# Reordering the prologue of a two-layer attention kernel: transposes of z one tile ahead, x requested one tile sooner

## The chip, the cores and the metric

The kernel runs on one core of one Trainium2 chip. The metric is the device time of the whole program in microseconds (us), the median of several runs. All arithmetic is in 32-bit floats. The engines have short names in the profile: PE is TensorE (matmuls and transposes; PEld its weight loads), DVE is VectorE, ACT is ScalarE, POOL is GpSimd, SP is SyncE, whose queue issues most of the DMAs. Each engine works through its own instructions in the order in which the program gives them, and waits where one of them needs the result of another engine or a buffer that is still in use.

## The reference

`x` is 128 x 256 x 256 (rows s, positions i, channels), `z` is 256 x 256 x 128. Two layers follow each other; cut to what matters here:

```python
# layer 0: x = x + attention0(group_norm(x), z)
m_norm = layer_norm(m)                       # m = group_norm(x)
z_norm = layer_norm(z, eps=1e-5)             # over the 128 channels of z
q, k, v = m_norm @ Wq.T, m_norm @ Wk.T, m_norm @ Wv.T      # 8 heads of 32
b = (z_norm @ Wb.T).transpose(0, 3, 1, 2)[:, None]          # a bias for each head, i, j
scores = einsum('bsihc,bsjhc->bshij', q, k) * scale + b
p = softmax(scores)
# ... times v, gate, output matrix
# layer 1: x = x + attention1(group_norm(x)), banded, 4 heads of 64
```

`_gn` needs mean and variance of x over all rows and positions for each of 32 groups of channels, so all of x has to be read before layer 0 can start on its first row. The bias `b` is the same for all 128 rows s, so it is made once.

## The kernel before: the prologue

Before the main loop of layer 0 there is a prologue. It reads z in 16 tiles (`zjobs`, 2 MB each) and x in 8 blocks (4 MB each, `nga` is 8). For each tile of z: VectorE takes the variance of each row (`z_front`) and GpSimd turns it into 1/std by a power of -0.5; TensorE transposes the tile, ScalarE copies the transposed parts out of PSUM, and TensorE multiplies them with the weights of the bias (`z_back`, `z_project`). The mean need not be subtracted: the weights are centred instead. When two tiles (64 columns) are through, the result is transposed back into `ps_k`, VectorE multiplies it with 1/std, and ScalarE takes the exponential (`z_exp`), because the main loop multiplies by exp(b). For each block of x VectorE sums moments (`x_block`). Comments marked `#:` are added here.

```python
    def z_load(b, i0, parts=1):
        zt = pz.tile([P, IB, CZ], F32, name="zt", tag="zt", bufs=3)   #: three buffers
        ...
            nc.sync.dma_start(zt[:, part]..., z_rows[...])
        return zt

    def z_front(b, i0, zt):
        nonlocal zrs
        st = pz.tile([P, IB, 3], F32, name="zst", tag="zst", bufs=2)
        for i in range(0, IB, 2):                       #: 16 instructions
            if i % (IB // 4) == 0 and i:
                mark(i // (IB // 4))                    #: other work between the quarters, see plan
            nc.vector.bn_stats(...)
        at = i0 % IS
        if at == 0:
            zrs = pz.tile([P, IS], F32, name="zrs", tag="zrs", bufs=3)
        rs = zrs[:, at : at + IB]
        nc.vector.tensor_scalar(rs, st[:, :, 2], 1.0 / CZ, 1e-5, ALU.mult, ALU.add)
        nc.gpsimd.tensor_tensor(rs, rs, mhalf[:, :IB], ALU.pow)
        return zt, zrs

    def z_back(b, i0, zt, rs):
        nonlocal turned
        at = i0 % IS
        for j in range(at // 16, (at + IB) // 16):      #: two halves of a tile
            zTs = []
            for g in range(4):
                ps_t = pps.tile([P, 512], F32, name="ps_t", tag="zT", bufs=3)
                ...
                for a in range(4):
                    nc.tensor.transpose(ps_t[:, a * P : (a + 1) * P], zt[:, i + a, :], ident)
                zT = pz.tile([P, 512], F32, name="zT", tag="zT", bufs=10)
                nc.scalar.copy(zT, ps_t)
                zTs.append(zT)
            z_project()                                 #: of the half before
            turned = (b, i0 - at, rs, j, zTs)

    def z_project():
        ...
        for g in range(4):
            nc.tensor.matmul(ps_b[...], wbz[:, j]..., zTs[g], start=(j == 0), stop=(j == 3))
        if j == 1:
            z_exp()
        if j < 3:
            return
        bT = pz.tile([P, 512], F32, name="bT", tag="bT", bufs=2)
        nc.scalar.copy(bT, ps_b)
        ps_k = pps.tile([P, 4, 4, 4, H], F32, name="ps_k", tag="keys", bufs=1)
        for a in range(4):
            nc.tensor.transpose(ps_k[:, a]..., bT[:, a * P : (a + 1) * P], ident)
        bt = pz.tile([P, IS, H], F32, name="bt", tag="bt", bufs=2)
        for j in range(4):
            nc.vector.tensor_tensor(bt[...], ps_k[...], bcast(rs...), ALU.mult)
        weighed.append((b, i0, bt))

    def x_block(j):
        xa = px.tile([P, GA * NB, C], F32, name="xa", tag="xa", bufs=2)   #: two buffers
        nc.sync.dma_start(xa, x[j * GA : (j + 1) * GA]...)
        for g in range(0, G, 2):                        #: 16 instructions
            nc.vector.bn_stats(st0[:, j, g : g + 2, :]..., group_pairs(xa, g))
```

The work between the quarters of `z_front`: during tiles 1 and 6 it is steps of preparing the weights. After the last block of x (`ended`, tile 8) it is the plan below; a key gives how many tiles after that one, and after which quarter. `begin` and the two `next(steps)` make the moments of x (`gps` and `gps2` are small matmuls that average over the partitions, `rs_l` the root that GpSimd takes), `take`, `norm` and `weigh` start on the first rows of layer 0.

```python
    plan = {
        (0, 4): begin, (1, 1): lambda: next(steps), (1, 3): lambda: next(steps), (1, 4): take, (2, 3): norm,
        (3, 4): weigh,
        (5, 3): lambda: now.send(nc.scalar),            #: 1/std of the first rows to DRAM
        (6, 4): lambda: now.turn([mm("ps_x") for _ in range(KC)]),
        (7, 2): lambda: now.fetch(nc.scalar),           #: and back, on all partitions
        (7, 4): lambda: now.normal(),                   #: xnT, on GpSimd
    }
```

```python
    behind, nx, n = None, 0, 0
    prepare = weights()
    with tc.manual_schedule():                          #: each engine keeps the order of the program
        zts = [z_load(*zjobs[0], 2)]
        load(8)                                         #: small loads of weights, ScalarE's queue
        zts.append(z_load(*zjobs[1]))
        for n, job in enumerate(zjobs):
            front = z_front(*job, zts.pop(0) if zts else z_load(*job))
            if n == 0:
                next(prepare)
                next(prepare)
            else:
                load(4)
                if n == 1:
                    next(prepare)
            if behind is not None:
                z_back(*behind)                         #: of the tile before
            behind = (*job, *front)
            if nx < n and nx < nga:
                x_block(nx)
                nx += 1
                if nx == nga:
                    ended = n
            mark(4)
        assert not plan
        z_back(*behind)
        z_project()
        z_exp()
        now.project("qT", 0)                            #: then the main loop begins
        now.project("kT", 0)
        ...
```

Of the kernel before, what the change touches and what calls it, by code (L numbers as in the profile page):

```python
# [9 lines left out]
F32 = mybir.dt.float32  # L10
# [6 lines left out]
P = 128  # L17
# [4 lines left out]
def bcast(ap, axis, n):  # L22

    ap = ap.unsqueeze(axis)
    shape = list(ap.shape)
    shape[axis] = n
    return ap.broadcast_to(shape)
# [746 lines left out]
def fast_kernel(  # L774
# [28 lines left out]
    H = wbT.shape[1]  # L803
# [24 lines left out]
    queued = []  # L828

    def load(n):  # L830
        for _ in range(min(n, len(queued))):
            nc.scalar.dma_start(*queued.pop(0))
# [98 lines left out]
    for a in range(KC):  # L931
        for h in range(H1):
            n = P // H1
# [5 lines left out]
    for h in range(H1):  # L939
        n = P // H1  # L940
# [22 lines left out]
    def group_pairs(src, g):  # L963

        return src[:, :, g * GE : (g + 2) * GE].rearrange("p n (h e) -> p n e h", h=2)
# [30 lines left out]
    pps = tc.alloc_tile_pool(name="pre_ps", bufs=2, space=PSUM)  # L996

    def mm(name):
        return ps_mm.tile([P, 512], F32, name=name, tag="mm")
# [73 lines left out]
    nga = S // GA  # L1073
# [7 lines left out]
    zjobs = [(b, i) for b in range(NB) for i in range(0, I, IB)]  # L1081
# [3 lines left out]
    def z_load(b, i0, parts=1):  # L1085

        zt = pz.tile([P, IB, CZ], F32, name="zt", tag="zt", bufs=3)
        for u in range(parts):
            part = slice(u * IB // parts, (u + 1) * IB // parts)
            nc.sync.dma_start(  # L1090
                zt[:, part].rearrange("p (u b) c -> p u (b c)", b=NB),
                z_rows[b, :, (i0 + part.start) // NB : (i0 + part.stop) // NB, :],
            )
        return zt

    def z_front(b, i0, zt):
        nonlocal zrs

        st = pz.tile([P, IB, 3], F32, name="zst", tag="zst", bufs=2)
        for i in range(0, IB, 2):  # L1100
            if i % (IB // 4) == 0 and i:
                mark(i // (IB // 4))
            nc.vector.bn_stats(
                st[:, i : i + 2, :].rearrange("p i f -> p (i f)"),
                zt[:, i : i + 2, :].rearrange("p i c -> p c i"),
# [4 lines that stand above are left out]
        rs = zrs[:, at : at + IB]  # L1110
        nc.vector.tensor_scalar(rs, st[:, :, 2], 1.0 / CZ, 1e-5, ALU.mult, ALU.add)
        nc.gpsimd.tensor_tensor(rs, rs, mhalf[:, :IB], ALU.pow)
        return zt, zrs

    def z_back(b, i0, zt, rs):

        nonlocal turned
        at = i0 % IS
        for j in range(at // 16, (at + IB) // 16):
# [3 lines that stand above are left out]
                i = (4 * j + g) * 4 - at  # L1123
# [3 lines that stand above are left out]
                nc.scalar.copy(zT, ps_t)  # L1127
                zTs.append(zT)
            z_project()
            turned = (b, i0 - at, rs, j, zTs)  # L1130

    def z_project():
        nonlocal turned, ps_b
        if turned is None:
            return
        (b, i0, rs, j, zTs), turned = turned, None
        if j == 0:
            ps_b = pps.tile([P, 512], F32, name="ps_b", tag="bias", bufs=1)
        for g in range(4):
            nc.tensor.matmul(  # L1140
                ps_b[32 * g : 32 * (g + 1), :], wbz[:, j].rearrange("p a h -> p (a h)"), zTs[g],
                start=(j == 0), stop=(j == 3),
            )
        if j == 1:
            z_exp()
        if j < 3:
            return
        bT = pz.tile([P, 512], F32, name="bT", tag="bT", bufs=2)
        nc.scalar.copy(bT, ps_b)
        ps_k = pps.tile([P, 4, 4, 4, H], F32, name="ps_k", tag="keys", bufs=1)  # L1150
        for a in range(4):
            nc.tensor.transpose(
                ps_k[:, a].rearrange("p g j h -> p (g j h)"), bT[:, a * P : (a + 1) * P], ident
            )
        bt = pz.tile([P, IS, H], F32, name="bt", tag="bt", bufs=2)
        for j in range(4):
            q = slice(j * 16, (j + 1) * 16)
            nc.vector.tensor_tensor(
                bt[:, q, :].rearrange("p (g a) h -> p g a h", g=4), ps_k[:, :, :, j, :].rearrange("p a g h -> p g a h"),
                bcast(rs[:, q].rearrange("p (g a) -> p g a", g=4), 3, H), ALU.mult,  # L1160
            )
        weighed.append((b, i0, bt))

    def z_exp():

        while weighed:
            b, i0, bt = weighed.pop()
            for h in range(H):
                nc.scalar.activation(
                    eb[:, h, :, b * P + i0 // NB : b * P + (i0 + IS) // NB],  # L1170
                    bt[:, :, h].rearrange("p (u b) -> p b u", b=NB), AF.Exp, bias=bz_r[:, h : h + 1],
                )

    def x_block(j):
        xa = px.tile([P, GA * NB, C], F32, name="xa", tag="xa", bufs=2)
        nc.sync.dma_start(xa, x[j * GA : (j + 1) * GA].rearrange("s i c -> (s i) c").rearrange("(p n) c -> p n c", p=P))
        for g in range(0, G, 2):
            nc.vector.bn_stats(st0[:, j, g : g + 2, :].rearrange("p g f -> p (g f)"), group_pairs(xa, g))

# [273 lines left out]
    def pair(p):  # L1453
        return Pair(p) if p < NP else Nobody()

    turned, weighed = None, []
    zrs = ps_b = la = lb = ps_s = ps_o = M0 = R0 = None
    now = nxt = nn = None

# [22 lines left out]
    def weigh():  # L1482
# [6 lines left out]
# [3 lines that stand above are left out]
        (5, 3): lambda: now.send(nc.scalar),  # L1492
        (6, 4): lambda: now.turn([mm("ps_x") for _ in range(KC)]),
        (7, 2): lambda: now.fetch(nc.scalar),
        (7, 4): lambda: now.normal(),
    }
    ended = None

    def mark(quarter):
        if n == 1 and quarter < 4 or n == 6:  # L1500
            next(prepare, None)
        if ended is not None:
            plan.pop((n - ended, quarter), nothing)()


    behind, nx, n = None, 0, 0
    prepare = weights()
    with tc.manual_schedule():
        zts = [z_load(*zjobs[0], 2)]
        load(8)  # L1510
        zts.append(z_load(*zjobs[1]))
        for n, job in enumerate(zjobs):
            front = z_front(*job, zts.pop(0) if zts else z_load(*job))
            if n == 0:
                next(prepare)
                next(prepare)
            else:
                load(4)
                if n == 1:
                    next(prepare)  # L1520
            if behind is not None:
                z_back(*behind)
            behind = (*job, *front)
            if nx < n and nx < nga:
                x_block(nx)
                nx += 1
                if nx == nga:
                    ended = n
            mark(4)
        assert not plan  # L1530
        z_back(*behind)
        z_project()
        z_exp()
        now.project("qT", 0)
        now.project("kT", 0)
        for f in ("centre", "scale"):
            getattr(nxt, f)()
        for r in range(2):
            nxt.moments(r)
# [111 lines left out]
    with tc.tile_pool(name="l1", bufs=2) as sb, tc.tile_pool(  # L1651
        name="l1s", bufs=4
    ) as sm, tc.tile_pool(name="ps1_mm", bufs=2, space=PSUM) as ps_mm, tc.tile_pool(
        name="ps1_s", bufs=1, space=PSUM
# [236 lines left out]
@with_exitstack  # L1891
def mixer_kernel(ctx, tc, *args):

    nc = tc.nc
    keep = ctx.enter_context(tc.tile_pool(name="verdict", bufs=1))
    verdict = keep.tile([1, 1], mybir.dt.int32, name="verdict")
    fast_kernel(tc, *args, verdict)
    again = nc.values_load(verdict[0:1, 0:1], min_val=0, max_val=1)
    with tc.If(again > 0):
        general_kernel(tc, *args)  # L1900
# [53 lines left out]
```

## Time and profile before

| | |
|---|---|
| time, median of 3 runs | 3370.63 us (3367.43 to 3371.21) |
| profiled span | 3366.7 us, granted TensorE clock 0.983 |
| TensorE busy | 3221.6 us, 96% |
| VectorE busy | 2024.1 us, 60% |
| ScalarE busy | 1463.3 us, 43% |
| GpSimd busy | 1975.2 us, 59% |
| last block of x done | 161.1 us after the start |
| first scores of the main loop | 239.8 us after the start |

A line of the timeline reads: start and length in us, engine, source line, operation, tile written and tile read, shapes, the number of instructions merged, and in brackets how long the engine had been idle before it and what ended that. `SPq` is the queue of the SP engine: its lines are DMA requests, and their length is the time of asking, not of the transfer. In the view by windows, each engine has its busy time and, in brackets, its number of instructions; behind them are the granted clock, the busy share of the DMA engines and the rate.

### The profile page before, as it was taken

How to read it: one execution, taken by the hardware profiler on the slowest of the kernel's cores; microseconds unless marked ns; L12 is line 12 of the kernel's file. 1: busy time of each engine (PE TensorE's matmuls, PEld its weight loads, DVE VectorE, ACT ScalarE, POOL GpSimd, SP SyncE). 2: the span in 40 equal slices, each digit the busy share in tenths (PEclk: the TensorE clock that was granted, in tenths of full speed). 3: DMA queues.
4: the chain of work that ended last, by engine and by line, in shares of the span. 5: the costliest groups of instructions: out<-in, count | busy, mean ns of one | idle time of the engine just before them, and what ended most of it. 6: DMA issues, size and time to landing. Idle time of an engine off the chain costs nothing. (4 is left out here: it accounts for less than half of the span.)

```text
span 3366.7 us, 81193 instructions
## 1 busy us (share of the span) xinstructions
PE 3221.6 (96%) x35158; PEld 2032.1 (60%) x35158; DVE 2024.1 (60%) x3218; ACT 1463.3 (43%) x2121; POOL 1975.2 (59%) x1377
## 2 busy tenths in 40 slices
PE   5389999999999999999999998899999999999998
PEld 3245555555555555555555554567767777677676
DVE  7966666666666666666666666366544444443456
ACT  2264444444444444444444443344444444444443
POOL 2378787777777787887777874333333333333332
PEclk8699999999999999999999999999999999999999
DMA  9951212221222222122212221211211211212111
GB/s 351 367 136 43 72 49 73 74 73 48 73 74 60 55 71 68 48 73 74 74 49 73 74 63 45 68 58 53 64 53 52 65 53 55 62 52 62 56 57 53
DMA packets 198831, 262.91 MB, mean 78 GB/s; under 512 B 46304, under 2 KB 147552, under 8 KB 197312
## 3 DMA queue, kind: packets, MB, share of 16 engines
q1 hardware_dynamic: 193392, 254.72, 24.8%
q8 instruction: 279, 4.57, 0.7%
q10 hardware_dynamic: 5072, 2.90, 0.3%
q14 instruction: 88, 0.72, 0.1%
HBM read 188.82 MB, written 68.75 MB: 77 GB/s over the span
## 5 line engine op out<-in xcount | busy, mean ns | idle before, releaser
L1344 POOL TENSOR_TENSOR eboth<-e 128x512 f32<-128x512 f32 x512 | 640.4, 1272 | 389.4 <-DVE e L1339 389.4
L1339 DVE TENSOR_TENSOR e<-ps_sc,eb 128x1024 f32<-128x1024 f32 x512 | 603.0, 1219 | 316.4 <-ACT ps_sc L1330 227.2
L1330 ACT ACTIVATE ps_sc<-ps_sc 128x1024 f32<-128x1024 f32 x512 | 492.8, 1006 | 507.4 <-PE ps_sc L1323 507.4
L1743 POOL TENSOR_TENSOR e<-e,bw 128x384 f32<-128x384 f32 x256 | 259.6, 1037 | 443.5 <-ACT e L1741 443.5
L1704 PE MATMUL ps_p<-xgT,w_in 128*128 128x512 f32 x1024 | 468.1, 600 | 0.1
L1696 POOL TENSOR_TENSOR xt<-xt,bout_r 128x1024 f32<-128x1024 f32 x64 | 152.0, 2376 | 378.4 <-PE ps_x L1693 375.1
L1796 DVE TENSOR_TENSOR yo<-ps_y,xt 128x512 f32<-128x512 f32 x128 | 88.4, 691 | 380.0 <-PE ps_y L1792 380.0
L1704 PEld LDWEIGHTS ps_p<-xgT,w_in 128*128 128x128 f32 x1024 | 188.5, 190 | 199.0 <-issue 165.6
L1323 PE MATMUL ps_sc<-qT,kT 32*128 32x256 f32 x4096 | 293.7, 400 | 2.1 <-ACT kT L1293 2.1
L1354 PE MATMUL ps_ov<-e,v 128*32 128x256 f32 x4096 | 274.1, 385 | 0.5 <-DVE oT L1368 0.5
L1289 PE MATMUL ps_p<-xnT,wq 128*128 128x512 f32 x512 | 254.1, 618 | 0.7 <-POOL xnT L1276 0.6
L1289 PE MATMUL ps_p<-xgT,wg 128*128 128x512 f32 x512 | 253.9, 618 | 0.0
L1792 PE MATMUL ps_y<-w_out,oT 128*128 128x256 f32 x1024 | 250.1, 387 | 2.6 <-DVE oT L1777 2.6
L1396 PE MATMUL ps_y<-wo,oT 128*128 128x256 f32 x1024 | 243.9, 381 | 7.1 <-POOL oT L1386 7.1
L1396 PEld LDWEIGHTS ps_y<-wo,oT 128*128 128x128 f32 x1024 | 195.7, 191 | 88.1 <-issue 59.7
L1323 PEld LDWEIGHTS ps_sc<-qT,kT 32*128 32x128 f32 x4096 | 185.4, 184 | 94.4 <-issue 70.5
L1304 PE MATMUL ps_v<-wv,xnT 128*128 128x256 f32 x1024 | 242.1, 379 | 0.0
L1289 PE MATMUL ps_p<-xnT,wk 128*128 128x512 f32 x512 | 240.6, 592 | 0.0
L1719 PE MATMUL ps_v<-w_in,xgT 128*128 128x256 f32 x1024 | 231.8, 379 | 0.0
L1774 DVE RECIPROCAL rv<-odd 128x256 f32<-128x256 f32 x128 | 224.4, 1753 | 4.4
L1719 PEld LDWEIGHTS ps_v<-w_in,xgT 128*128 128x128 f32 x1024 | 194.4, 190 | 53.5 <-issue 30.1
L1304 PEld LDWEIGHTS ps_v<-wv,xnT 128*128 128x128 f32 x1024 | 189.6, 190 | 50.9 <-issue 31.1
(163 smaller groups left out, 4978.1 us busy)
## 6 DMA issues: line engine op xcount, KB each, us to landing
xa<-in_x_dram SPq DMA_DIRECT2D x8, 4096.0 KB
xt<-in_x_dram SPq DMA_DIRECT2D x64, 512.0 KB
rvb<-rsum SPq DMA_DIRECT2D x256, 128.0 KB
x<-xo SPq DMA_DIRECT2D x16, 2048.0 KB
xt<-x SPq DMA_DIRECT2D x64, 512.0 KB
out_dram<-yo SPq DMA_DIRECT2D x63, 512.0 KB
zt<-in_z_dram SPq DMA_DIRECT2D x15, 2048.0 KB
rs_r<-rs_d SPq DMA_DIRECT2D x63, 256.0 KB
```

The source lines that it names most:

```text
L1289: nc.tensor.matmul(ps, w[:, k, m * P : (m + 1) * P], getattr(self, src)[:, k, :], start=(k == 0), stop=(k == KC - 1),)
L1304: nc.tensor.matmul(self.ps_v[:, b * C : (b + 1) * C], self.xnT[:, k, t * P : (t + 1) * P], wv[:, k, :], start=(k == 0), stop=(k == KC - 1),)
L1323: nc.tensor.matmul(self.pss[q // 2][:, q % 2, b, :], self.kT[rs, c, r * I + b * P : r * I + (b + 1) * P], self.qT[rs, c, r * I : (r + 1) * I],
L1330: nc.scalar.activation(self.pss[a], self.pss[a], AF.Exp)
L1339: nc.vector.tensor_tensor(e, pss[a], eb[:, h : h + 2], ALU.mult)
L1344: nc.gpsimd.tensor_tensor(t, es[a][:, :, 0, :], es[a][:, :, 1, :], ALU.add)
L1354: nc.tensor.matmul(ov[q * D0 : (q + 1) * D0, :], self.v[:, r, b, h * D0 : (h + 1) * D0], es[q // 2][:, q % 2, b, :], start=(b == 0), stop= ...
L1396: nc.tensor.matmul(self.ps_y[:, b * C : (b + 1) * C], self.oT[r][:, k, b * P : (b + 1) * P], wo[:, k, :], start=(k == 0), stop=(k == KC - 1),)
L1704: nc.tensor.matmul(ps, w_in[:, k, n * C + m * P : n * C + (m + 1) * P], self.xgT[:, k, :], start=(k == 0), stop=(k == KC - 1),)
L1719: nc.tensor.matmul(ps[:, b * C : (b + 1) * C], self.xgT[:, k, t * P : (t + 1) * P], w_in[:, k, 2 * C : 3 * C], start=(k == 0), stop=(k == ...
L1743: nc.gpsimd.tensor_tensor(e[:, q], e[:, q], bcast(bw.rearrange("p b w -> p (b w)"), 1, KC), ALU.mult)
L1792: nc.tensor.matmul(ps[:, b * C : (b + 1) * C], self.oT[r][:, k, b * P : (b + 1) * P], w_out[:, k, :], start=(k == 0), stop=(k == KC - 1),)
```

## The change

The change keeps all instructions and reorders them. TensorE and ScalarE no longer work on the tile behind VectorE but on the one ahead: `z_back` of tile n+1 stands before `z_front` of tile n. 1/std is then not known yet when the tile is projected, so the projected pair is set aside (`projected`, in one of now two PSUM buffers), and the products with 1/std come in `z_scale`, a tile later, on VectorE. The block of x is requested one tile sooner, apart from its use. The aim is that the buffers of z come free as soon as VectorE is done with them, that neither TensorE nor ScalarE stands in the way of the requests, and that at the end of the prologue little is left after the last tile.

```diff
@@ z_front
         nc.gpsimd.tensor_tensor(rs, rs, mhalf[:, :IB], ALU.pow)
-        return zt, zrs
-
-    def z_back(b, i0, zt, rs):
+        if at:
+            roots.append(zrs)
+
+    def z_back(b, i0, zt):
 ...
-            turned = (b, i0 - at, rs, j, zTs)
+            turned = (b, i0 - at, j, zTs)
@@ z_project
-        if j == 1:
-            z_exp()
         if j < 3:
             return
         bT = pz.tile([P, 512], F32, name="bT", tag="bT", bufs=2)
         nc.scalar.copy(bT, ps_b)
-        ps_k = pps.tile([P, 4, 4, 4, H], F32, name="ps_k", tag="keys", bufs=1)
+        ps_k = pps.tile([P, 4, 4, 4, H], F32, name="ps_k", tag="keys", bufs=2)
         for a in range(4):
             nc.tensor.transpose(...)
+        projected.append((b, i0, ps_k))
+
+    def z_scale():
+
+        b, i0, ps_k = projected.pop(0)
+        rs = roots.pop(0)
         bt = pz.tile([P, IS, H], F32, name="bt", tag="bt", bufs=2)
         for j in range(4):
 ...
-    def x_block(j):
+    def x_load(j):
         xa = px.tile([P, GA * NB, C], F32, name="xa", tag="xa", bufs=2)
         nc.sync.dma_start(xa, ...)
+        return xa
+
+    def x_block(j, xa):
         for g in range(0, G, 2):
 ...
-    behind, nx, n = None, 0, 0
+
+    n, nz = 0, len(zjobs)
     prepare = weights()
     with tc.manual_schedule():
         zts = [z_load(*zjobs[0], 2)]
         load(8)
         zts.append(z_load(*zjobs[1]))
+        xas = [x_load(0)]
         for n, job in enumerate(zjobs):
-            front = z_front(*job, zts.pop(0) if zts else z_load(*job))
+            if n:
+                if n < nga:
+                    xas.append(x_load(n))
+                if n + 1 < nz:
+                    zts.append(z_load(*zjobs[n + 1]))
+                load(4)
+            if n > 1 and n + 1 < nz:
+                z_back(*zjobs[n + 1], zts[n + 1])
+            if n + 1 == nz:
+                z_project()
+            z_exp()
+            z_front(*job, zts[n])
+            if n < 2:
+                next(prepare)
             if n == 0:
                 next(prepare)
-                next(prepare)
-            else:
-                load(4)
-                if n == 1:
-                    next(prepare)
-            if behind is not None:
-                z_back(*behind)
-            behind = (*job, *front)
-            if nx < n and nx < nga:
-                x_block(nx)
-                nx += 1
-                if nx == nga:
+            if n == 1:
+                for a in range(3):
+                    z_back(*zjobs[a], zts[a])
+            if n > 1 and n % 2 == 0:
+                z_scale()
+            if 0 < n <= nga:
+                x_block(n - 1, xas[n - 1])
+                if n == nga:
                     ended = n
             mark(4)
-        assert not plan
-        z_back(*behind)
-        z_project()
+        assert not plan and not queued
+        z_scale()
         z_exp()
         now.project("qT", 0)
```

More of the change, by code (lines that the diff above doesn't have):

```diff
@@ L1135, in z_project @@
             return
-        (b, i0, rs, j, zTs), turned = turned, None
+        (b, i0, j, zTs), turned = turned, None
         if j == 0:
@@ L1454, in pair @@
         return Pair(p) if p < NP else Nobody()
-    turned, weighed = None, []
+    turned, roots, projected, weighed = None, [], [], []
     zrs = ps_b = la = lb = ps_s = ps_o = M0 = R0 = None
```

## The prediction

> **What bounds the kernel now.** I first cut the span in three with the busy-time view by windows, at two moments taken from the timeline: 161.1, when VectorE ends the last block of x, and 239.8, when the main loop's first scores start on TensorE.
>
> ```profile
> core 0: us, PE busy (x) PEld busy (x) DVE busy (x) ACT busy (x) POOL busy (x), PEclk, DMA share, GB/s
> 0.00:161.10 161.10, 69.89 (x428) 47.82 (x428) 136.98 (x338) 43.77 (x92) 51.89 (x24) 0.79 1.00 369
> 161.10:239.80 78.70, 61.03 (x434) 37.40 (x434) 52.19 (x168) 49.93 (x113) 56.11 (x15) 0.91 0.57 156
> 239.80:3366.70 3126.90, 3090.68 (x34298) 1946.86 (x34298) 1834.89 (x2715) 1369.56 (x1916) 1867.15 (x1338) 1.00 0.21 61
> ```
>
> The last row is everything that the change leaves alone: TensorE is busy 3090.7 of 3126.9 us, so it starts later or earlier with the prologue and keeps its length. Only the first 239.8 us, 7% of the span, can move. In the first part the DMA share is 1.00 and VectorE is busy 85%; in the second no engine is full, so there it is waits.
>
> For the first part I read the timeline of VectorE and of the SP queue, steps 4 and 5:
>
> ```profile
> 79.99 5.41 DVE L1103 BATCH_NORM_STATS2 zst<-zt 128x6 f32<-128x256 f32 x16
> 80.09 7.20 SPq L1176 DMA_DIRECT2D xa<-in_x_dram  x1
> ...
> 87.25 9.61 DVE L1178 BATCH_NORM_STATS2 st<-xa 128x6 f32<-128x512 f32 x16 [1.64 <-DMA xa<-in_x_dram]
> 87.34 0.43 SPq L1090 DMA_DIRECT2D zt<-in_z_dram  x1
> 96.78 5.35 DVE L1103 BATCH_NORM_STATS2 zst<-zt 128x6 f32<-128x256 f32 x16
> 96.89 6.02 SPq L1176 DMA_DIRECT2D xa<-in_x_dram  x1
> ...
> 103.01 0.39 SPq L1090 DMA_DIRECT2D zt<-in_z_dram  x1
> ```
>
> A step of VectorE is 5.5 us on a tile of z (5.4 and the 0.18 of zrs) and 9.7 on a block of x, plus 0.9 for the products every second step. The x request at 80.09 follows the end of block 2 at 80.0: it waited for that buffer. By count it is x4, and the z request after it z6, two tiles ahead. The completion counts of the DMAs in the trace give the landings: z4 76.6, x3 87.2, z5 93.2, x4 102.9, z6 108.9, x5 118.7, z7 124.7, x6 135.2, z8 141.2, x7 151.0. The queue works in order and without a pause: an x takes 9.8 us (up to 10.6), a z 6.0, a pair 16.0. VectorE's step is 15.2 or 16.1, so both limits lie on each other.
>
> For the second part I read TensorE's timeline and the SP queue:
>
> ```profile
> 140.13 1.14 PE L1140 MATMUL ps_b<-zT,wbz 128*32 128x512 f32 x8
> 164.25 0.63 PE L972 MATMUL gps_l<-mean_l,avg 128*128 128x32 f32 x2 [22.98 <-DVE mean_l L971]
> 166.35 0.63 PE L981 MATMUL gps_l<-d_l,avg 128*128 128x32 f32 x2 [1.47 <-DVE d_l L979]
> 166.80 3.65 PE L1125 MATMUL ps_t<-ident,zt 128*128 128x128 f32 x16
> ```
>
> ```profile
> 175.31 0.37 SPq L1090 DMA_DIRECT2D zt<-in_z_dram  x1
> ```
>
> The matmuls of x's moments stand ahead of the transposes of z8 in TensorE's order and wait 23 us for VectorE. So z8's buffer comes free only at 175, and z11, asked for there, lands at 184.1; the DMA has had nothing since 165.5. After that every z request waits for TensorE's transposes, 7 us apart. This is the wait that the change aims at.
>
> **The Trainium skill.** "DMA: Bandwidth & Descriptors", section "Anatomy of one DMA — SWDGE (gpsimd) path", gives a DMA a fixed cost of about 2.0 us, mostly completion. The queue here is another path, but the trace shows a like cost: z11 on an idle queue took 8.8 us from request to landing, against 6.0 behind others, so 2.8 us. Its section "Rules for kernel authors" says to issue early so that this cost overlaps; the kernel before does. "TensorE: Matmul & The Clock Gate", section "What's actually happening", says that an idle TensorE falls to half its clock; 16 transposes after the 23 us wait took 3.65 us against 2.0 later.
>
> **The change, part by part.** No arithmetic is added or dropped: 512 transposes, 128 copies, 16 powers of 5.43 us, 32 products and 128 exponentials stay. Only orders change.
>
> (a) The order of requests. Before it was z(n), x(n-1), z(n+1), x(n); after it is x(n), z(n+1), x(n+1), z(n+2). x(n) still needs the buffer of x(n-2), free only at the end of step n-1, so x goes out no sooner than before in the steady state. But z(n+1) now stands behind it, where z(n+2) stood. The queue loses one z of lead. When z(n) has landed and step n-1 ends, nothing is in flight, and the DMA stands still until the next x is asked for.
>
> I follow this by hand, with x 9.8, z 6.0 and 2.8 for a restart. z1 lands at 23.9 and x0 at 34.1 as before; then x1 44.3 and z2 50.4 instead of 40.0. VectorE, done with block 0 at 45.2, waits until 50.5. In even steps the products follow z_front and need ps_k of the pair before, which hangs on the first half of the transposes of the same tile: by the trace 3.65 + 1.6 + 0.6 + 0.8 us after landing (cold), so 1.1 us after z_front ends. An even step is then 5.5 + 1.1 + 0.9 + 9.7 = 17.2 us, an odd one 15.2. The x asked for at the end of an even step meets an idle queue: 12.6 us, and z 6.0 behind it. Two steps thus take 17.2 + 12.6 + 6.0 = 35.8 us; before, two were 32.1. From 50.5: step 4 starts at 87.0 (80.0 before; the small loads add 0.5), step 6 at 123.0, step 8, with 2.3 us of weights in step 6, at 160.1 (before 146.0). Step 8 ends at 160.1 + 17.2 = 177.3; before it was 161.1. Loss: 16.2 us.
>
> (b) After that end (call it 0) TensorE is ahead and z10 and z11 are already there: the 20 us without DMA are gone. But there is a new wait. The second matmul of the moments is issued inside z_front of tile 9, and the transposes of z10 now stand before it on TensorE; they start after the first moments matmul at 3.1 and take 9.4 (166.80 to 176.20 for such a tile in the trace). VectorE needs the result for rs_l at 7.6 and gets it at about 13.7: 6 us of waiting. Then GpSimd is the pace: rs_l until 19.5, power 9 until 24.9, centre and scale (4.8) until 29.7, power 10 35.1, power 11 40.6, root 41.6, power 12 47.0, and products of a pair wait for its power. VectorE: z_front(12) ends at 38.9, products at 41.6, z_front(13) 47.1, (14) 52.6, products 53.6, (15) 59.1. z15, asked for at 38.9, is there at 48. Power 15 ends at 64.7, xnT 67.3, the q and k products 71.1 and the copy of kT 71.9. Scores start at 72.0; before it was 239.8 - 161.1 = 78.7. Gain: 6.7 us.
>
> Sum: +16.2 - 6.7 = +9.5 us, so 3380. Errors of (a) are more likely towards less loss (an x on an idle queue may start sooner than a z, and the first loads may come sooner, since x0 is asked for at once), so I take 2 to 3 us off: 3377.5 us.
>
> **The rivals.** First, the intended one: the DMA keeps its pace of 16.0 us a pair, step 8 ends near 161 or 163, and (b) counts alone, or more if the moments matmul finds TensorE free; that is -7 to -14 us, 3357 to 3364. For it: the trace shows the SP queue held 16.9 us by TensorE at the place removed. Against it: in steps 4 to 8 no such wait ever left the DMA idle. Second, the late small loads: they are now issued on ScalarE's queue behind a tile's copies and share completion counters with x and z; in the trace x3 waited to 72.5 for one issued at 56.0. If an x waits like this on an emptier queue, add 5 to 10 us: 3385. Third, GpSimd's powers are not the pace of the end, because z15 lands late or the root-square row is fetched late (its request is now behind the last exponentials on ScalarE): up to 5 us more.
>
> **Range and chances.** The three put the time between 3362 and 3388. 2% is 67 us, more than a quarter of the prologue; no account of mine reaches it either way.
>
> **What would show it.** In the changed profile: VectorE waiting 2 to 4 us for zt before every even z_front, and about 5 before tile 2; DMA share under 1 in the first 170 us; the last block of x ending at 172 to 178; a wait of about 6 us of VectorE for gps2 in tile 9; no gap in TensorE that holds a z request; first scores at 246 to 250. I am wrong if block 7 ends by 165, which would mean that the lead of one z tile was not needed, or if the main loop's length moves from 3126.9 by over 3 us.

## The result

| | before | after |
|---|---|---|
| time, median of 5 runs each | 3370.14 us (3367.43 to 3371.21) | 3401.39 us (3400.55 to 3402.42) |
| profiled span | 3366.7 us | 3399.6 us |
| last block of x done | 161.1 us | 200.7 us |
| from there to the first scores | 78.7 us | 70.9 us |
| first scores of the main loop | 239.8 us | 271.6 us |
| main loop and all behind it | 3126.9 us | 3128.0 us |

The ratio is 1.0094, with a 95% interval of 1.008 to 1.0109: the changed kernel is 31 us slower. The prediction was 3377.5 us with a range to 3388, so the time lies 13 us above the range.

First the view by windows of the kernel after, cut at the same two events as before: the end of the last block of x and the first scores.

```profile
core 0: us, PE busy (x) PEld busy (x) DVE busy (x) ACT busy (x) POOL busy (x), PEclk, DMA share, GB/s
0.00:200.70 200.70, 85.89 (x528) 59.54 (x528) 138.16 (x342) 53.41 (x109) 51.89 (x24) 0.77 0.84 307
200.70:271.60 70.90, 48.31 (x335) 29.05 (x335) 48.72 (x161) 41.17 (x96) 56.34 (x15) 0.90 0.44 143
271.60:3399.60 3128.00, 3091.12 (x34298) 1946.86 (x34298) 1836.71 (x2717) 1369.50 (x1916) 1866.94 (x1338) 0.99 0.21 61
```

The reader is to see three things. The last row has hardly moved. The second row is 7.8 us shorter than before. The first row is 39.6 us longer with the same VectorE work (138.2 us, before 137.0), and the DMA share, 1.00 before, is 0.84. Something stops both the transfers and VectorE, for more than twice the 16.2 us that the prediction gave this part.

The view of VectorE's waits in the first 272 us of the kernel after gives, in order, the instruction that waited, what it waited for, and then the total in us, the number of times and the longest:

```profile
DVE zst L1104 <- DMA zt<-in_z_dram: 36.6, 7, 6.6
DVE bout_r L1071 <- PE ps_bo L1069: 21.9, 1, 21.9
...
DVE rs_l L984 <- PE gps_l L981: 4.7, 1, 4.7
```

Of the first line, 15.2 us are waits for the first two tiles, which the kernel before has too (16.1 us); the other 21.4 us, before tiles 2, 4, 6 and 8, are the lost lead of z that the prediction had. The second line is new: one single wait of 21.9 us for the small matmul `ps_bo`, which before cost 0.6 us. It belongs to the last step of preparing the weights: VectorE makes `bv_w`, TensorE multiplies it with `w_out` into `ps_bo`, and in the next step VectorE adds that to `bout_r`. These steps run between the quarters of `z_front` of tile 6. In the kernel before, TensorE is idle when `bv_w` is made and runs `ps_bo` at once, ahead of the transposes; first TensorE's timeline there, then VectorE's:

```profile
115.09 2.08 PE L1069 MATMUL ps_bo<-w_out,bv_w 128*128 128x256 f32 x4 [29.86 <-DVE bv_w L1066]
116.96 3.62 PE L1125 MATMUL ps_t<-ident,zt 128*128 128x128 f32 x16
```

```profile
117.21 0.42 DVE L1071 TENSOR_TENSOR bout_r<-bout_r,ps_bo 128x256 f32<-128x256 f32 x1 [0.64 <-PE ps_bo L1069]
```

VectorE's timeline of the kernel after around it:

```profile
125.23 1.42 DVE L1104 BATCH_NORM_STATS2 zst<-zt 128x6 f32<-128x256 f32 x4 [5.20 <-DMA zt<-in_z_dram]
...
127.44 0.48 DVE L1066 TENSOR_SCALAR bv_w<-ones,bv_c 128x128 f32<-128x128 f32 x2
127.84 1.41 DVE L1104 BATCH_NORM_STATS2 zst<-zt 128x6 f32<-128x256 f32 x4
151.19 0.42 DVE L1071 TENSOR_TENSOR bout_r<-bout_r,ps_bo 128x256 f32<-128x256 f32 x1 [21.94 <-PE ps_bo L1069]
151.53 2.73 DVE L1104 BATCH_NORM_STATS2 zst<-zt 128x6 f32<-128x256 f32 x8
```

And TensorE's timeline of the kernel after in the same stretch:

```profile
133.32 1.06 PE L1142 MATMUL ps_b<-zT,wbz 128*32 128x512 f32 x8
142.14 3.65 PE L1127 MATMUL ps_t<-ident,zt 128*128 128x128 f32 x16 [7.76 <-DMA zt<-in_z_dram]
...
150.02 1.13 PE L1069 MATMUL ps_bo<-w_out,bv_w 128*128 128x256 f32 x4
```

`bv_w` is there at 127.9, and TensorE is done with z6 at 134.4. But `z_back` of tile 7 now stands ahead of `z_front` of tile 6 in the program, so `ps_bo` stands behind all transposes of z7, and z7 lands at 142.0. TensorE idles 7.76 us for it, then works 7.9 us on z7, and only then on `ps_bo`. VectorE, which had half of tile 6 still to do and a landed block of x behind it, stands for 21.94 us. In the prediction's own words of (a), x(n) needs the buffer of x(n-2); so the queue of the SP engine stands too:

```profile
120.07 0.33 SPq L1182 DMA_DIRECT2D xa<-in_x_dram  x1
120.50 0.38 SPq L1090 DMA_DIRECT2D zt<-in_z_dram  x1
164.81 0.33 SPq L1182 DMA_DIRECT2D xa<-in_x_dram  x1
```

These are x6, z7 and x7. Between z7's landing at 142.0 and the request of x7 at 164.81, which is the end of block 5, the DMA engines have nothing to do, as the view by windows shows with a share of 0.00:

```profile
142.20:164.70 22.50, 8.95 (x52) 5.94 (x52) 13.47 (x31) 4.40 (x8) 5.43 (x1) 0.65 0.00 0
```

The wait is passed on to the transfers.

### The profile page after: what moved, and what is told of

Same layout as the page of the kernel before. It is cut to its first block, busy times and chain, and to the rows that moved or that the text cites. A ratio compares the mean times of both kernels' runs of the same rounds, so it can differ in the third digit from the quotient of the medians.

```text
span 3399.6 us, 81186 instructions
## 1 busy us (share of the span) xinstructions
PE 3225.3 (95%) x35158; PEld 2035.4 (60%) x35158; DVE 2023.6 (60%) x3218; ACT 1464.1 (43%) x2121; POOL 1975.2 (58%) x1377
## 5 line engine op out<-in xcount | busy, mean ns | idle before, releaser
L1348 DVE TENSOR_TENSOR e<-ps_sc,eb 128x1024 f32<-128x1024 f32 x512 | 603.0, 1219 | 315.6 <-ACT ps_sc L1339 226.0
```

The costliest lines, as they stand in the source:

```text
L1348: nc.vector.tensor_tensor(e, pss[a], eb[:, h : h + 2], ALU.mult)
```

## The experiments

Theory A: the loss is the sum of two independent parts, the lost lead of z (16 to 18 us) and the wait for `ps_bo` (22 us), less the gain at the end (7 to 8 us). Rival B: `ps_bo` runs late because its operands come late from ScalarE's queue of small loads, and its place on TensorE does not matter. Rival C: the lead does not matter by itself, the loss of the transfers' pace comes from TensorE working ahead. Rival D: the end part is set by something other than GpSimd's powers. The first four runs are made for A and C: the two parts apart, and then both undone.

**1. The sum with `ps_bo` two tiles later.** In the changed kernel, the addition to `bout_r` moves from the second quarter of tile 6 to the first quarter of tile 8; nothing else.

```diff
-        if n == 1 and quarter < 4 or n == 6:
+        if n == 1 and quarter < 4 or n in (6, 8) and quarter == 1:
             next(prepare, None)
```

> The kernel after, with only the add of ps_bo into bout_r taken from tile 6 to tile 8, so that VectorE no longer waits in tile 6 for a matmul that stands behind the transposes of z7. Theory (that wait of 21.9 us counts in full): 3380 us, 21 to 22 below the kernel after; last block of x done at 179 instead of 200.7. Rival (the wait only hid time in which the DMA would have been waited for): 3390 or more.

Measured: 3379.72 us, ratio to the kernel before 1.0025 (1.0015 to 1.0035). Its view by windows:

```profile
0.00:178.70 178.70, 86.40 (x528) 59.47 (x528) 138.06 (x342) 53.25 (x109) 51.85 (x24) 0.78 0.94 343
178.70:249.40 70.70, 48.16 (x332) 29.26 (x332) 48.55 (x160) 41.21 (x96) 56.30 (x15) 0.90 0.47 148
249.40:3377.40 3128.00, 3090.76 (x34298) 1946.63 (x34298) 1837.93 (x2717) 1368.61 (x1916) 1865.60 (x1338) 1.00 0.22 61
```

The first row is 22.0 us shorter than in the kernel after, as long as the wait was; the other rows stay. VectorE's addition now follows without a wait:

```profile
163.64 0.40 DVE L1071 TENSOR_TENSOR bout_r<-bout_r,ps_bo 128x256 f32<-128x256 f32 x1
```

So the 21.94 us counted in full. What is left is the kernel that the prediction had worked out: last block of x at 178.7 (predicted 177.3), 70.7 us from there (predicted 72.0), first scores at 249.4 (239.8 + 9.5 = 249.3).

**2. The order of requests alone.** The kernel before, with its `z_back` behind, but x and z asked for in the order of the change.

```diff
+        xas = [x_load(0)]                               #: after z_load of tile 1
         for n, job in enumerate(zjobs):
-            front = z_front(*job, zts.pop(0) if zts else z_load(*job))
+            if n:
+                if n < nga:
+                    xas.append(x_load(n))
+                if n + 1 < len(zjobs):
+                    zts.append(z_load(*zjobs[n + 1]))
+            front = z_front(*job, zts[n])
 ...
-                x_block(nx)
+                x_block(nx, xas[nx])
```

> The kernel before, with only the requests in the order of the change: x(n), then z(n+1). TensorE stays behind VectorE. Theory (the lost lead of one tile of z costs time by itself): 3377 us, 4 to 12 above before, DMA share below 1 and VectorE waiting for z in the even steps. Rival (the order of requests is free, all of the loss comes from TensorE's order): 3370, same as before.

Measured: 3384.36 us, ratio 1.004 (1.0025 to 1.0054), 13 us more than before, where 4 to 12 more and 3377 us were expected. By windows:

```profile
0.00:173.90 173.90, 69.35 (x428) 47.70 (x428) 137.34 (x338) 43.76 (x92) 51.89 (x24) 0.79 0.95 344
173.90:254.60 80.70, 61.36 (x432) 37.59 (x432) 50.75 (x171) 49.91 (x113) 56.12 (x15) 0.90 0.55 147
```

The first part is 12.8 us longer than before without TensorE ahead, and the DMA share falls to 0.95: the lost lead costs by itself, and rival C falls. VectorE waits for z 13 times in the first 260 us, 49.3 us in all (before: 7 times in the first 240 us, 28.0 us), the longest 8.06 us before tile 2. In run 1, with TensorE ahead, the same part is 17.6 us longer than before. VectorE's waits account for the 4.8 us between the two runs: 2.4 us are waits for `ps_k`, which run 2 does not have in this part, and the waits for z from tile 2 on are 20.3 us in run 1 and 17.8 in run 2. The end part, 80.7 us, does not become shorter than before (78.7), since TensorE is still behind.

**3. The lead given back, `ps_bo` left where it is.** In the changed kernel z is again asked for two tiles ahead of its use.

```diff
         xas = [x_load(0)]
+        zts.append(z_load(*zjobs[2]))
         for n, job in enumerate(zjobs):
             if n:
                 if n < nga:
                     xas.append(x_load(n))
-                if n + 1 < nz:
-                    zts.append(z_load(*zjobs[n + 1]))
+                if 1 < n < nz - 2:
+                    zts.append(z_load(*zjobs[n + 2]))
 ...
                 for a in range(3):
                     z_back(*zjobs[a], zts[a])
+                zts.append(z_load(*zjobs[3]))
```

> The kernel after, with the requests again one tile of z further ahead (x(n), then z(n+2)); the wait for ps_bo in tile 6 stays. Theory: no waits for z in tiles 2 to 5, but 17 to 18 us of waiting for ps_bo, as z7 still lands near 125; last block of x done near 179, 3381 us. Rival (ps_bo waits only because z7 comes late, and goes with the lead): 3363.

Measured: 3382.45 us, ratio 1.0034 (1.0021 to 1.0046). VectorE's timeline:

```profile
113.87 1.44 DVE L1104 BATCH_NORM_STATS2 zst<-zt 128x6 f32<-128x256 f32 x4
133.78 0.42 DVE L1071 TENSOR_TENSOR bout_r<-bout_r,ps_bo 128x256 f32<-128x256 f32 x1 [18.47 <-PE ps_bo L1069]
```

The wait is still 18.5 us although z7 is asked for a tile sooner, since VectorE also comes to tile 6 sooner (111.3 instead of 125.2). An earlier request does not cure the order on TensorE.

**4. Both.** The edits of runs 1 and 3 together.

```diff
-        if n == 1 and quarter < 4 or n == 6:
+        if n == 1 and quarter < 4 or n in (6, 8) and quarter == 1:
 ...
+        zts.append(z_load(*zjobs[2]))
 ...
-                if n + 1 < nz:
-                    zts.append(z_load(*zjobs[n + 1]))
+                if 1 < n < nz - 2:
+                    zts.append(z_load(*zjobs[n + 2]))
 ...
+                zts.append(z_load(*zjobs[3]))
```

> Both of the above: requests one tile of z further ahead, and the add of ps_bo in tile 8. Theory: last block of x done at 161 to 162 as before, the rest 71 us as in the kernel after, against 78.7 before: 3363 us, 7 below before. Rival (with TensorE ahead the front of the prologue is slower for another reason): 3370 or more.

Measured: 3361.89 us, ratio 0.9973 (0.9961 to 0.9984), faster than the kernel before by 9.5 us. By windows:

```profile
0.00:161.70 161.70, 83.24 (x500) 57.78 (x504) 137.88 (x342) 50.94 (x105) 51.85 (x24) 0.81 0.99 367
161.70:231.70 70.00, 50.55 (x368) 29.73 (x360) 48.92 (x161) 43.23 (x101) 56.31 (x15) 0.93 0.56 177
```

The first row is the first row of before again (161.1 us, share 1.00), and the second keeps the gain of working ahead. The four runs with TensorE ahead form a square:

| median time, us | addition to `bout_r` in tile 6 | in tile 8 |
|---|---|---|
| z asked for one tile ahead | 3401.4 (the change) | 3379.7 (run 1) |
| z asked for two tiles ahead | 3382.5 (run 3) | 3361.9 (run 4) |

Along the rows the wait for `ps_bo` is worth 21.7 and 20.6 us, down the columns the lead 18.9 and 17.8 us. The two add up within 1.1 us: theory A stands. (The change was not timed together with runs 1, 3 and 4; the kernel before took 3370.1 us beside the change and 3371.4 beside these runs, so a difference of 1 us between the two groups means nothing.)

**5. The second small matmul freed too.** Run 4 still has the wait that the prediction had named in (b), of `rs_l` for the second matmul of the moments. Here `z_back` of tile 10 comes after `z_front` of tile 9 instead of ahead of it.

```diff
-            if n > 1 and n + 1 < nz:
+            if n > 1 and n + 1 < nz and n != nga + 1:
                 z_back(*zjobs[n + 1], zts[n + 1])
 ...
             z_front(*job, zts[n])
+            if n == nga + 1:
+                z_back(*zjobs[n + 1], zts[n + 1])
```

> The kernel with more lead and ps_bo in tile 8, and besides the transposes of z10 put behind the second moments matmul of x (behind z_front of tile 9). Theory (the same kind of wait, 3.5 us before rs_l in that kernel, and GpSimd's chain of powers starts that much sooner): 3358 us, 3 to 4 below that kernel. Rival (the end is paced by VectorE or by z's landing, not by the start of rs_l): no gain, 3362.

Measured: 3359.21 us, ratio 0.9961 (0.9947 to 0.9975). VectorE's timeline in run 4 and then in run 5:

```profile
173.22 0.19 DVE L984 TENSOR_SCALAR rs_l<-gps_l 128x32 f32<-128x32 f32 x1 [3.56 <-PE gps_l L981]
```

```profile
168.27 2.76 DVE L1104 BATCH_NORM_STATS2 zst<-zt 128x6 f32<-128x256 f32 x8
170.94 0.19 DVE L984 TENSOR_SCALAR rs_l<-gps_l 128x32 f32<-128x32 f32 x1
```

The wait is gone, and the first scores come at 228.6 instead of 231.7. By the profile that is 3.1 us: the end part is 66.0 us instead of 70.0, and the part before it 0.9 us longer. The intervals of the two ratios overlap, so the times alone do not part runs 4 and 5. Against the kernel before both are faster. Run 5 leaves nothing out and is the version to keep: no kernel here that does all of the work has a lower time (run 8 below has the same).

**6. The matmul moved, not the addition.** This is for rival B. In the changed kernel the step that makes `bv_w` and issues `ps_bo` is put ahead of the transposes of z7; the addition stays in tile 6.

```diff
-        if n == 1 and quarter < 4 or n == 6:
+        if n == 1 and quarter < 4 or n == 6 and quarter == 1:
             next(prepare, None)
 ...
+            if n == 6:
+                next(prepare)
             if n > 1 and n + 1 < nz:
                 z_back(*zjobs[n + 1], zts[n + 1])
```

> The kernel after, with only the scaling of the weights and the ps_bo matmul moved ahead of the transposes of z7 in tile 6; the add stays in tile 6. Theory (the matmul's place in TensorE's order, behind transposes that wait for z7, is the whole of the wait): 3378 to 3381 us. Rival (the wait is for the last small loads, bv_c and w_out, which now come late on ScalarE's queue): little gain, 3395 or more.

Measured: 3388.21 us, ratio 1.0046 (1.0031 to 1.0062), 7 us above what theory A asked for. TensorE's timeline, and then VectorE's:

```profile
125.60 3.65 PE L1127 MATMUL ps_t<-ident,zt 128*128 128x128 f32 x16 [12.70 <-DMA zt<-in_z_dram]
...
133.70 1.07 PE L1142 MATMUL ps_b<-zT,wbz 128*32 128x512 f32 x8
134.69 1.13 PE L1069 MATMUL ps_bo<-w_out,bv_w 128*128 128x256 f32 x4
142.67 3.65 PE L1127 MATMUL ps_t<-ident,zt 128*128 128x128 f32 x16 [6.84 <-DMA zt<-in_z_dram]
```

```profile
121.14 0.48 DVE L1066 TENSOR_SCALAR bv_w<-ones,bv_c 128x128 f32<-128x128 f32 x2
125.49 1.42 DVE L1104 BATCH_NORM_STATS2 zst<-zt 128x6 f32<-128x256 f32 x4 [3.87 <-DMA zt<-in_z_dram]
135.86 0.42 DVE L1071 TENSOR_TENSOR bout_r<-bout_r,ps_bo 128x256 f32<-128x256 f32 x1 [8.95 <-PE ps_bo L1069]
```

`bv_w` is made at 121.1, but `ps_bo` is free of the transposes of z7 only to stand behind those of z6, which wait for z6's landing at 125.5 just as VectorE does. It runs at 134.69, straight behind the work on z6 and without a wait of its own, so its operands were there, 15 us before it runs in the kernel after: rival B falls. My own expectation had missed the same thing one tile earlier. The miss is useful, since it gives a second size of the wait: with 0, 8.95 and 21.94 us of it (runs 1, 6 and the change) the first scores come at 249.4, 258.2 and 271.6, that is +8.8 and +22.2 us.

**7. Is GpSimd the pace of the end?** For rival D: run 5, with the powers of tiles 9 to 15 replaced by a product. This kernel leaves out the 1/std of those tiles, so their bias is scaled wrongly; only its time is read.

```diff
-        nc.gpsimd.tensor_tensor(rs, rs, mhalf[:, :IB], ALU.pow)
+        nc.gpsimd.tensor_tensor(rs, rs, mhalf[:, :IB], ALU.pow if n <= nga else ALU.mult)
```

> The kernel of the first of these three runs, with the powers of tiles 9 to 15 left out: a product of the same tiles in their place on GpSimd. Theory (GpSimd's chain of powers sets the pace of the end): first scores 8 to 11 us sooner, 3347 to 3351. Rival (the landing of z or VectorE sets it): at most 3 us, and then only by the last power, 3355.

Measured: 3355.9 us, ratio 0.9949 (0.9934 to 0.9964): the first scores come 3.3 us sooner than in run 5 (225.3 instead of 228.6), where 8 to 11 us were expected if GpSimd alone set the pace. The size is that of the rival. Of the 3.3 us, 0.8 are there before the first cheap power: the root for `rs_l` starts at 170.42 instead of 171.21. GpSimd's timeline in run 5 and then in run 7:

```profile
198.87 16.21 POOL L1113 TENSOR_TENSOR zrs<-zrs,mhalf 128x32 f32<-128x32 f32 x3
215.98 5.43 POOL L1113 TENSOR_TENSOR zrs<-zrs,mhalf 128x32 f32<-128x32 f32 x1 [0.90 <-DVE zrs L1112]
221.37 2.49 POOL L1285 TENSOR_TENSOR xnT<-xgT,rs_r 128x512 f32<-128x512 f32 x2
```

```profile
210.82 0.25 POOL L1113 TENSOR_TENSOR zrs<-zrs,mhalf 128x32 f32<-128x32 f32 x1 [6.10 <-DVE zrs L1112]
216.95 2.49 POOL L1285 TENSOR_TENSOR xnT<-xgT,rs_r 128x512 f32<-128x512 f32 x2 [5.88 <-DMA rs_r<-rs_d]
```

In run 5 three powers stand in a row, a fourth follows after 0.9 us, and then `xnT` without a wait: GpSimd is the pace there. With cheap powers z_front of tile 15 starts at 205.1 instead of 210.3, 5 us sooner, but `xnT` starts only 4.4 us sooner, after a wait of 5.88 us for `rs_r`, the row of 1/std that comes back from DRAM. So the powers are the pace, and some 4 us behind them the fetch takes over, which the third rival of the prediction had named. What the recorded rival of this run had named, the landing of z or VectorE, did not take over.

**8. The end shortened by order.** Run 5, with `rs_r` fetched on the SP queue, `xnT` ahead of the last power on GpSimd, and the q and k products ahead of the last products with 1/std.

```diff
-        (7, 2): lambda: now.fetch(nc.scalar),
-        (7, 4): lambda: now.normal(),
+        (7, 2): lambda: now.fetch(),
+        (7, 3): lambda: now.normal(),
 ...
+        now.project("qT", 0)
+        now.project("kT", 0)
         z_scale()
         z_exp()
-        now.project("qT", 0)
-        now.project("kT", 0)
```

> The kernel with more lead, ps_bo in tile 8 and gps2 first, and besides its end reordered: rs_r fetched on SP's queue, xnT on GpSimd ahead of the power of the last tile, the first q and k ahead of the last products and exponentials. Nothing is left out. Theory (first scores hang on power 15, then xnT, then q and k, in a row): xnT at 216 instead of 221.4, first scores near 223 instead of 228.6, 3354 to 3356 us. Rival (the landing of rs_r or the exponentials of the last pair, now later, hold the main loop's first tiles): 3359 or more.

Measured: 3359.22 us, ratio 0.997 (0.9959 to 0.9982): nothing gained over run 5 (0.9961, and the intervals overlap), as the rival had it. The first scores come at 226.0, 2.6 us sooner (the end part is 61.8 us instead of 66.0, and the part before it 1.6 us longer), but what follows them takes 3131.5 us instead of 3127.7. The timeline of all engines in this run shows why:

```profile
225.97 1.15 PE L1332 MATMUL ps_sc<-qT,kT 32*128 32x256 f32 x16 [0.78 <-ACT kT L1302]
...
226.36 0.49 DVE L1164 TENSOR_TENSOR bt<-ps_k,zrs 128x128 f32<-128x128 f32 x2 [8.51 <-POOL zrs L1113]
226.89 2.46 ACT L1175 ACTIVATE eb<-bt,bz_r 128x64 f32<-128x64 f32 x8 [0.97 <-DVE bt L1164]
...
229.25 1.90 ACT L1339 ACTIVATE ps_sc<-ps_sc 128x1024 f32<-128x1024 f32 x2
...
232.91 2.35 DVE L1348 TENSOR_TENSOR e<-ps_sc,eb 128x1024 f32<-128x1024 f32 x2
```

The last power is now the last work of the prologue. The scores are there, but their exponentials stand on ScalarE behind the last ones of z, and VectorE's first product of the loop starts at 232.91, later than in run 5 (230.92). The last power, products and exponentials went from before the scores to behind them, and the loop paid it back.

Not tried: more buffers for x and z instead of another order.

## Why the prediction was wrong

**The step that failed is the term for the weights of tile 6 in (a)**: "step 8, with 2.3 us of weights in step 6, at 160.1". It took the preparation as VectorE time and missed that its last step contains a round trip over TensorE. In the changed kernel that round trip costs 21.94 us. The prediction had found the same kind of wait in (b), for the second matmul of the moments ("the transposes of z10 now stand before it on TensorE"), and applied it to that one place only. Going through the changed program, from tile 2 on, for every matmul whose result VectorE needs inside a `z_front` finds `ps_bo` in tile 6 just as it finds the one in tile 9; the first was not examined. None of the three rivals had it either; the second, late small loads, was about a request of x that waits, and not about `ps_bo`.

**(a), the order of requests, was right apart from that.** With `ps_bo` out of the way the last block of x ends at 178.7 (run 1), predicted 177.3; the loss is 17.6 us, predicted 16.2. The kernel after shows the pattern that was asked for: VectorE waits for z before tiles 2, 4, 6 and 8 for 5.39, 6.55, 5.20 and 4.24 us. "About 5 before tile 2" is right; "2 to 4 us" for the others is too small. The term mis-sized is the double step of 35.8 us: in run 1 tiles 2 and 3 took 39.0 us (50.14 to 89.09), 4 and 5 took 37.2 (to 126.33), and 6 and 7, with the weights, 36.0 (to 162.30), which is less than the 37.1 that the prediction gave them. The difference lies in the transfers: after x was asked for, it and the z behind it were there in 21.4, 20.2 and 18.7 us, where the prediction had 18.6. In the first two of these stretches small loads of ScalarE's queue moved too, in the third none; that they are the cause was not tried. The sum of the prediction also has a slip: 50.5 + 3 x 35.8 + 0.5 + 2.3 is 160.7 and not 160.1. (Its 128 exponentials are 64 in the trace; nothing rests on them.) In time, the square gives the lead as 17.8 to 18.9 us. The advice of the Trainium skill that the prediction used ("DMA: Bandwidth & Descriptors", section "Rules for kernel authors": issue early) agrees, with that number.

**(b), the end, was right.** Counted from the end of the last block in the kernel after, `rs_l` comes at 12.5 us (predicted 13.7), after a wait of 4.65 us (predicted 6); GpSimd is done with its power at 18.2 (19.5), with power 11 at 39.5 (40.6), and the first scores are at 70.9 (72.0). The gain is 7.8 us instead of 6.7. That GpSimd's powers are the pace is shown by run 7, within the limit shown there: only about 4 us lie between them and the fetch of `rs_r`, and the powers' own share of what was gained is 2.5 us of 3.3.

**The sum was right, and the correction of it was not.** The text had +9.5 us and 3380; run 1, which is the change without the wait for `ps_bo`, measured 3379.7 (8.3 us more than the kernel before beside it). That they meet so closely is in part luck: (a) lost 1.4 us more than predicted, and (b) gained 1.3 us more (8.0 in run 1 instead of 6.7). The 2 to 3 us taken off "towards less loss" had nothing measured behind them, and (a) as a whole went the other way. The range of 3362 to 3388 covered the rivals that had been thought of, and had no room for a wait of a kind already known at a place not looked at.

**The first rival** ("the DMA keeps its pace", 3357 to 3364) is what the change was meant to be. It fell as a prediction of this change, but its size is that of runs 4 and 5, 3361.9 and 3359.2 us: with the lead kept and the two small matmuls moved out of the way, the intention holds.

**The main loop** kept its length: 3128.0 us against 3126.9, within the 3 us allowed.

## What to carry to other kernels

When an engine is made to work one tile ahead, a small result that another engine needs back from it can now stand behind work on data that has not landed. List all such round trips in the stretch concerned, and for each ask when the tile ahead of it in the queue will arrive; here two small matmuls cost 21.94 and 4.65 us, and moving the use of the first two tiles later, and the long work of the second behind it, removed both. A prefetch order is to be written down as "how many tiles are in flight when the consumer begins": moving a request up in the program while another is put in front of it can reduce that number, and here one tile of it cost 18 to 19 us.

## What the runs showed of the hardware that was not expected

Writing the 1/std of the first rows to DRAM and reading it back is slow for its 128x4 values. In run 8 the write was asked for at 205.03. The read of it, first in the SP queue with no other request since 197.17, went out only at 213.46, and the view of that queue's waits names the write as what released it (15.9 us is how long the queue had been idle):

```profile
SPq L1266 <- DMA rs_d<-lrs: 15.9, 1, 15.9
```

That is 8.4 us for 2 kB, longer than the 6.0 us of a 2 MB tile of z behind others. The moving of the bytes is the small part: by the DMA records of this trace its 512 pieces of 4 bytes had gone by 206.3, and the completion counts of the write came from 211.6 to 213.4. Why they came so late was not tried. The read itself was there at 218.3, 4.9 us after its request. In run 5 the row is there at 217.6, 3.8 us before `xnT` starts, so the fetch stands only some 4 us behind GpSimd's powers; and asking on another queue brought little, since the read still has to wait for the write.
